# Pairs of heads on one 32-row strip of keys, and seven PSUM banks for the last element's second attention

## The chip, the cores and the metric

The kernel runs on one core of one Trainium2 chip. The metric is device time in microseconds (us) of one execution; lower is better. Times of several executions are given by their median.

## The reference

The input is `x` of shape 8 x 512 x 256 (elements, tokens, features). Four layers with residuals follow each other; all are in fp32. Cut to what matters:

```python
x = x + attn_a(layernorm(x))   # per token: 16 heads, a causal 64 x 64 table of q_i * k_j in each head
x = x + ffn(layernorm(x))      # 256 -> 1024 gated, 1024 -> 1024 twice, 1024 -> 256
x = x + attn_b(layernorm(x))   # causal attention over the 512 tokens, 16 heads of 16 features
x = x + ffn(layernorm(x))      # the same weights again

def attn_b(x):                                  # the "second attention"
    q, k, v = split(x @ W_attn + b_attn, 3)     # 256 -> 3 * 256
    s = q @ k.T / 4                             # per head, keys after the query masked
    return (softmax(s) @ v) @ W_proj + b_proj
```

## The kernel before, in words

Two streams of work are woven into one program. Stream A is the first attention of all eight elements (class `AttentionA`): 512 steps, 64 for each element, most of them on VectorE and GpSimd, with an exponential on ScalarE (L818) and a few matmuls. Stream B is the rest of each element, one element behind A: `ffn`, `attention_b`, `ffn`, most of it on TensorE. The order of the instructions on each engine is the order in which the source issues them. B is a generator that yields the worth of each piece of its work in units of its own; the main loop issues pieces of B after each third of an A step until B has done `total / 64` units for each A step, with `total = 309.5` units for an element. A has no more steps when B begins with the last element (`b = 7`), which is therefore processed by B alone.

TensorE does all matmuls, ScalarE copies their products out of PSUM and takes exponentials. PSUM has eight banks, in three pools: `ps_f` with five (stream B), `ps_qv` with two (queries and values of A) and the one tile `bank` of `ps_a` (A's small products, in halves). SBUF blocks of 128 x 2048 for B come from the pool `hp` with seven buffers, weights of B from `hwp` with three.

`attention_b` of one element goes through these parts:

- **Queries and keys** (L1187, copied out at L1208). Each head has 16 features and gets a strip of 32 partitions (`SLOT`), half of it zeros, so 16 heads fill four groups of 128 partitions (`BG = 4`). For queries (`j = 0`) and for keys (`j = 1`) there are four products of 128 x 512 each, two matmuls (`c`) in each product. The keys' four products are issued one by one, each followed by its copy.
- **Values** (L1225, copied at L1228): four products of 128 x 256.
- **Scores** `scores(g, j)` for the group `g` of four heads and the block `j` of 128 keys, with the width `w = 512 - 128 j` of queries: four matmuls, one per head, on four 32-row strips of the array, into four PSUM banks (L1242); four small matmuls that add the causal mask (L1246); four exponentials on ScalarE (L1249) into the SBUF tile `eb`, of which there is one.
- **Values' products** `values(g, j)`: four matmuls, one per head, on four 32-column strips, that add into the PSUM tile `pyb` of the group (L1254). After the last `j` of a group ScalarE copies `pyb` to `ytb` (L1263).
- Then the sums of the exponentials divide, the heads are turned back and projected, and `x` is updated.

The loop over the 16 pairs `(g, j)` issues, for each pair, the values' products of the pair before and then the scores of this pair:

```python
for j in range(NT):
    if before is not None:
        values(*before)
    es = scores(g, j)
```

The weights of queries and keys (tile `wbqk`, 1 MB for an element) are prepared once in `later_weights`, kept in the DRAM tensor `wbqk_d`, and loaded again for each element (L954).

Of the kernel before, what the change touches and what calls it, by code (L numbers as in the profile page):

```python
# [9 lines left out]
F32 = mybir.dt.float32  # L10
# [6 lines left out]
P = 128  # L17
EPS = 1e-5
NEG = -1e30
NB, S, D = 8, 512, 256  # L20
NT = S // P
DC = D // P
# [4 lines left out]
GW = GH * C  # L27
# [6 lines left out]

BH, HD, SLOT = 16, 16, 32
BG = BH * SLOT // P

FH = 1024
MC = FH // P
HB = 2048  # L40
# [3 lines left out]
def general_path(ctx: ExitStack, tc: tile.TileContext, k, t):  # L44
# [29 lines left out]
    nc.sync.dma_start(s3_sb, t.s3.broadcast_to([P, D]))  # L74
    wbqk_sb = wp.tile([P, DC, 2, BG * P], F32, name="g_wbqk")
    nc.sync.dma_start(wbqk_sb, t.w_bqk.rearrange("(c p) j f -> p c j f", p=P))
    bbqk_sb = wp.tile([P, 2, BG], F32, name="g_bbqk")
    nc.sync.dma_start(bbqk_sb, t.b_bqk)
# [3 lines left out]
    nc.sync.dma_start(wbp_sb, t.w_bp.rearrange("(c p) f -> p c f", p=P))  # L82
    bq_scaled = wp.tile([P, BG], F32, name="g_bqs")
    nc.vector.tensor_scalar_mul(bq_scaled, bbqk_sb[:, 0, :], HD**-0.5)
# [125 lines left out]
    def attention_b(xt):  # L210
        xnt = normed_block(xt)
        qk = hp.tile([P, 2, BG, S], F32, tag="h", name="g_qkb")
        for j in range(2):
            for g in range(BG):
                pp = ps.tile([P, S], F32, tag="pf", name="g_pqkb")
# [69 lines left out]
def fast_path(ctx: ExitStack, tc: tile.TileContext, k, t, flag):  # L285

    nc = tc.nc
# [3 lines left out]
    dram = ctx.enter_context(tc.tile_pool(name="dram", bufs=1, space=bass.MemoryType.DRAM))  # L291
# [8 lines left out]
    ps_qv = ctx.enter_context(tc.tile_pool(name="ps_qv", bufs=2, space=bass.MemoryType.PSUM))  # L300
    ps_a = ctx.enter_context(tc.tile_pool(name="ps_a", bufs=1, space=bass.MemoryType.PSUM))
    ps_f = ctx.enter_context(tc.tile_pool(name="ps_f", bufs=5, space=bass.MemoryType.PSUM))
# [7 lines left out]
    def block(name, dtype=F32):  # L310

        return hp.tile([P, HB], dtype, tag="h", name=name)
# [49 lines left out]
    def less_row(w, c, row, p0):  # L362

        ps = ps_f.tile([P, 2 * GW], F32, tag="pf", name="pfit")[:, : w.shape[-1]]
        nc.tensor.matmul(ps, ident, w, start=True, stop=False)
        nc.tensor.matmul(ps, from_rows[p0 : p0 + 1, c, :], row, start=False, stop=True)
        return ps

    def fit_qkv(g):

        wqv, wk = fitted[g]
        rows = (
            (wqv, last_rows[0:1, g * 2 * GW : (g + 1) * 2 * GW], 0),
            (wk, last_rows[32:33, g * GW : (g + 1) * GW], 32),
        )
        for w, row, p0 in rows:
            pss = [less_row(w[:, c], c, row, p0) for c in range(DC)]
            yield
            for c, ps in enumerate(pss):
                nc.scalar.copy(w[:, c], ps)  # L380
            yield
        nc.sync.dma_start(wqv_d[g].rearrange("p (c f) -> p c f", c=DC), wqv)
        nc.sync.dma_start(wk_d[g].rearrange("p (c f) -> p c f", c=DC), wk)
# [52 lines left out]
        nc.vector.tensor_scalar(over[0:1, 0:2], over[0:1, 0:2], 1.0, None, ALU.is_gt)  # L436

    w3_d = dram.tile([P, HB], F32, name="w3_d")
    wbqk_d = dram.tile([P, HB], F32, name="wbqk_d")
    wbvp_d = dram.tile([P, 2 * DC * D], F32, name="wbvp_d")  # L440

    nc.gpsimd.memset(rows_of_1[:, D:], 1.0)
# [2 lines left out]
    def later_weights():  # L445


        for j, row in enumerate((t.bo, t.b_bp)):
            nc.sync.dma_start(biases[j][:, :D], row)
        for g in range(1, NG):  # L450
            yield from fit_qkv(g)

        wbqk = block("wbqk").rearrange("p (c f) -> p c f", c=DC)
        rows = block("rows")
        w3 = block("w3").rearrange("p (c f) -> p c f", c=MC)
        wbvp = block("wbvp")[:, : 2 * DC * D].rearrange("p (j c f) -> p j c f", j=2, c=DC)
        n_qk = 2 * BG * P
        s3 = rows[:, n_qk + D : n_qk + 2 * D]
        nc.sync.dma_start(s3, t.s3.broadcast_to([P, D]))
        nc.sync.dma_start(w3, t.w3.rearrange("(c p) f -> p c f", p=P))  # L460
        nc.sync.dma_start(wbqk, t.w_bqkb.rearrange("(c p) j f -> p c (j f)", p=P))
        nc.sync.dma_start(wbvp[:, 0], t.w_bvb.rearrange("(c p) f -> p c f", p=P))
        nc.sync.dma_start(wbvp[:, 1], t.w_bp.rearrange("(c p) f -> p c f", p=P))
        nc.sync.dma_start(rows[0:1, :n_qk], t.w_bqk[D - 1 : D].rearrange("o j f -> o (j f)"))
        nc.sync.dma_start(rows[0:1, n_qk : n_qk + D], t.w_bv[D - 1 : D])
        yield
        for c in range(0, MC, 2):
            pair = w3[:, c : c + 2, :]
            nc.gpsimd.tensor_tensor(pair, pair, s3.unsqueeze(1).to_broadcast(list(pair.shape)), ALU.mult)
            yield  # L470
        for w, off, width in ((wbqk, 0, 2 * GW), (wbqk, 2 * GW, 2 * GW), (wbvp[:, 0], 0, D)):
            row = rows[0:1, n_qk if width == D else off :][:, :width]
            pss = [less_row(w[:, c, off : off + width], c, row, 0) for c in range(DC)]
            yield
            for c, ps in enumerate(pss):
                nc.scalar.copy(w[:, c, off : off + width], ps)
            yield

        nc.sync.dma_start(w3_d, w3.rearrange("p c f -> p (c f)"))
        nc.sync.dma_start(wbqk_d, wbqk.rearrange("p c f -> p (c f)"))  # L480
        nc.sync.dma_start(wbvp_d, wbvp.rearrange("p j c f -> p (j c f)"))
        yield
        yield from bound_scores()
# [18 lines left out]
    bank = ps_a.tile([P, 2, GW], F32, name="bank")  # L502
# [674 lines left out]
    def attention_b(b, xt, nx, after):  # L1177
        yield from nx.wait(NT - 1)
        xnt = nx.t
        qk = [block(f"qkb_{b}_{j}").rearrange("p (g s) -> p g s", g=BG) for j in range(2)]  # L1180
        w = weights.take().rearrange("p (c j f) -> p c j f", c=DC, j=2)
        for j in range(2):
            pps = [None] * BG

            def products(g, toks):
                for c in range(DC):
                    nc.tensor.matmul(  # L1187
                        pps[g][:, toks],
                        w[:, c, j, g * P : (g + 1) * P],
                        xnt[:, c, toks],  # L1190
                        start=(c == 0),
                        stop=(c == DC - 1),
                    )

            if j == 0:

                for g in range(BG):
                    pps[g] = ps_f.tile([P, S], F32, tag="pf", name=f"pqkb_{b}_{j}_{g}")
                    products(g, most)
                    if g % 2:  # L1200
                        flush()
                        yield 2
                yield from nx.wait(NT)
            for g in range(BG):
                if j > 0:
                    pps[g] = ps_f.tile([P, S], F32, tag="pf", name=f"pqkb_{b}_{j}_{g}")
                products(g, slice(0, S) if j > 0 else last)
                nc.scalar.activation(qk[j][:, g, :], pps[g], AF.Copy, scale=HD**-0.5 if j == 0 else 1.0)  # L1208
                yield 1.8 if j > 0 else 0.6
            if j == 0:  # L1210
                weights.ahead()

        vs = block(f"vb_{b}").rearrange("p (i h s) -> p i h s", i=NT, h=BH)
        yts = block(f"ytb_{b}").rearrange("p (g q) -> p g q", g=BG)
        exps = block(f"eb_{b}").rearrange("p (h q) -> p h q", q=S)
        rest = block(f"yb_{b}")
        y2 = rest[:, : 2 * D].rearrange("p (n h d) -> p n h d", n=2, h=BH)
        yt2 = rest[:, 2 * D : 4 * D].rearrange("p (n c q) -> p n c q", n=2, c=DC)
# [16 lines left out]
        heads = range(P // SLOT)  # L1235
        slots = [slice(h * SLOT, (h + 1) * SLOT) for h in heads]

        def scores(g, j):
            keys, w = slice(j * P, (j + 1) * P), S - j * P
            scs = [ps_f.tile([P, S], F32, tag="pf", name=f"psb_{b}_{g}_{j}_{h}")[:, :w] for h in heads]  # L1240
            for h in heads:
                nc.tensor.matmul(  # L1242
                    scs[h], qk[1][slots[h], g, keys], qk[0][slots[h], g, j * P :], start=True, stop=False
                )
            for h in heads:
                nc.tensor.matmul(scs[h][:, :P], k.ident16, k.tmask16, start=False, stop=True)  # L1246
            es = [exps[:, h, :w] for h in heads]
            for h in heads:
                nc.scalar.activation(es[h], scs[h], AF.Exp)  # L1249
            return es  # L1250
# [14 lines left out]
        before = None  # L1265
        for g in range(BG):
            for j in range(NT):
                if before is not None:
                    values(*before)
                es = scores(g, j)  # L1270
                if j == 0:
                    yt = ps_f.tile([P, S], F32, tag="pf", name=f"pyb_{b}_{g}")
                before = (yt, g, j, es)
                yield 6 - j
# [81 lines left out]


    each = NT * NG * NU
    total = 309.5
    ET = mybir.EngineType  # L1360
    with tc.manual_schedule(engines={ET.PE, ET.DVE, ET.Activation, ET.Pool}):
        a = AttentionA()
# [4 lines left out]
        weights = None  # L1367
# [104 lines left out]
```

## Time and profile before

| | |
|---|---|
| median of 3 runs | 3988.24 us (3980.57 to 3991.68) |
| profiled execution, first to last instruction | 3990.8 us |
| the same execution's own time | not given apart; its span lies within the runs |
| mean granted TensorE clock | 0.849 |
| busy: TensorE, VectorE, GpSimd, ScalarE | 76%, 85%, 77%, 59% of the span |
| stream A's last output is copied by ScalarE at | 3687.1 us |
| second attention of the last element: first product of the queries | 3801.7 us |
| its last exponential; its last copy of `ytb` | 3871.8 us; 3872.9 us |

Times within the profile are us from its first instruction. The page of the profile lists groups of instructions by source line; the timeline lists single instructions or merged rows of equal ones, with the idle time of the engine before them and what ended it in brackets. One product of fp32 appears as two matmul records. The busy share is a mean over the whole span and hides the two stages: until 3687 us both streams run, after it B alone.

### The profile page before, as it was taken

How to read it: one execution, taken by the hardware profiler on the slowest of the kernel's cores; microseconds unless marked ns; L12 is line 12 of the kernel's file. 1: busy time of each engine (PE TensorE's matmuls, PEld its weight loads, DVE VectorE, ACT ScalarE, POOL GpSimd, SP SyncE). 2: the span in 40 equal slices, each digit the busy share in tenths (PEclk: the TensorE clock that was granted, in tenths of full speed). 3: DMA queues.
4: the chain of work that ended last, by engine and by line, in shares of the span. 5: the costliest groups of instructions: out<-in, count | busy, mean ns of one | idle time of the engine just before them, and what ended most of it. 6: DMA issues, size and time to landing. Idle time of an engine off the chain costs nothing.

```text
span 3990.8 us, 37932 instructions
## 1 busy us (share of the span) xinstructions
PE 3039.9 (76%) x12464; PEld 2055.2 (52%) x12464; DVE 3375.9 (85%) x3776; ACT 2341.3 (59%) x3156; POOL 3077.9 (77%) x3040
## 2 busy tenths in 40 slices
PE   5653487687877878678876878778787778778988
PEld 2231264365634656356643656346553556446847
DVE  7999988998899888998899988998989888996115
ACT  3444475576665675666755766666755767565342
POOL 6888878887888788887788887887888877886111
PEclk7556599798987988888987989879898889879999
DMA  8766777577776877768775877668776677767304
GB/s 229 182 137 137 159 197 158 124 191 189 199 154 139 196 191 178 148 163 202 200 157 118 208 186 194 149 142 213 174 190 143 160 182 206 158 129 211 116 28 169
DMA packets 118346, 669.24 MB, mean 168 GB/s; under 512 B 12662, under 2 KB 31865, under 8 KB 43643
## 3 DMA queue, kind: packets, MB, share of 16 engines
q0 software_dynamic: 78336, 570.46, 63.2%
q1 hardware_dynamic: 39804, 96.27, 6.7%
q8 instruction: 101, 1.65, 0.2%
q14 instruction: 105, 0.86, 0.1%
HBM read 254.07 MB, written 9.96 MB: 66 GB/s over the span
## 4 chain that ended last, share of the span: by engine, by line
DVE 38%; PE 18%; POOL 14%; DMA 13%; ACT 8%; issue 8%; SPq 0%; ACTq 0%; POOLq 0%; DVEq 0%
DVE red L865 15%; DMA w<-w 13%; DVE w L828 10%; PE ph L1140 5%; ACT w L818 4%; POOL w L804 3%; POOL w L839 3%; DVE ws L828 3%; PE pqkb L1187 3%; POOL acc L872 3%; DVE w L804 2%; DVE ws L804 2%; POOL h L1056 2%; POOL w L834 2%; DVE acc L876 2%
## 5 line engine op out<-in xcount | busy, mean ns | idle before, releaser
L818 ACT ACTIVATE w<-w 128x2048 f32<-128x2048 f32 x384 | 733.8, 1912 | 659.2 <-POOL w L804 461.3
L1140 PE MATMUL ph<-h,hidden 128*128 128x512 f32 x4096 | 1042.9, 411 | 72.4 <-POOL h L1056 42.9
L804 POOL TENSOR_TENSOR w<-k 128x1024 f32<-128x1024 f32 x512 | 1077.4, 2104 | 7.7 <-ACT k L782 7.1
L1140 PEld LDWEIGHTS ph<-h,hidden 128*128 128x128 f32 x4096 | 792.3, 195 | 275.3 <-POOL h L1056 53.8
L828 DVE TENSOR_TENSOR w<-w,qv 128x1024 f32<-128x1024 f32 x768 | 898.8, 1211 | 22.4 <-ACT w L818 22.4
L865 DVE TENSOR_REDUCE red<-w 128x128 f32<-128x1024 f32 (+1 forms) x384 | 601.3, 1566 | 178.0 <-DMA w<-w 93.6
L839 POOL TENSOR_TENSOR w<-w 128x1024 f32<-128x1024 f32 x256 | 643.7, 2514 | 82.9 <-DMA w<-w 82.3
L834 POOL DMA_DIRECT2D w<-w x384 | 337.9, 880 | 349.0 <-issue 121.1
L872 POOL TENSOR_TENSOR acc<-acc,red 128x256 f32<-128x256 f32 (+1 forms) x640 | 471.2, 736 | 142.7 <-DVE red L865 122.0
L865 DVE TENSOR_REDUCE red<-ws 128x256 f32<-128x2048 f32 (+1 forms) x256 | 435.4, 1742 | 0.0
L766 PE MATMUL qv<-wqv,xnta 128*128 128x512 f32 x512 | 299.7, 716 | 104.6 <-DVE ws L828 95.4
L1072 PE MATMUL pw<-xnt,gate 128*128 128x512 f32 (+2 forms) x1152 | 301.8, 422 | 21.7 <-ACT silu L1048 16.1
L828 DVE TENSOR_TENSOR ws<-ws,qv 128x1024 f32<-128x1024 f32 (+3 forms) x512 | 294.3, 635 | 27.6 <-ACT ws L818 27.6
L804 DVE TENSOR_TENSOR w<-qv,k 128x1024 f32<-128x1024 f32 x256 | 301.1, 1218 | 3.6
L804 DVE TENSOR_TENSOR ws<-qv,k 128x1024 f32<-128x1024 f32 (+3 forms) x512 | 299.5, 646 | 0.2 <-issue 0.2
L888 PE MATMUL bank<-ident,acc 128*128 128x128 f32 x256 | 62.4, 333 | 284.5 <-ACT k L781 278.6
L818 ACT ACTIVATE ws<-ws 128x1920 f32<-128x1920 f32 x128 | 231.5, 1808 | 80.7 <-DVE ws L804 80.1
L1072 PEld LDWEIGHTS pw<-xnt,gate 128*128 128x128 f32 x1152 | 230.8, 215 | 76.2 <-ACT silu L1048 20.4
L1249 ACT ACTIVATE eb<-psb 128x256 f32<-128x256 f32 (+3 forms) x512 | 182.1, 443 | 139.1 <-PE psb L1246 138.6
L1166 PE MATMUL pof<-w,h 128*128 128x256 f32 x1024 | 244.9, 392 | 22.8 <-ACT h L1105 22.8
L1105 ACT ACTIVATE h<-ph,s_sb 128x512 fp32r<-128x512 f32 (+1 forms) x256 | 171.2, 688 | 151.1 <-PE ph L1140 149.7
L876 DVE RECIPROCAL acc<-acc 128x256 f32<-128x256 f32 x128 | 222.9, 1741 | 11.9 <-POOL acc L872 11.9
(149 smaller groups left out, 4846.4 us busy)
## 6 DMA issues: line engine op xcount, KB each, us to landing
w<-w POOLq DMA_DIRECT2D x384, 1024.0 KB, 7.8
hidden<-in_h POOLq DMA_DIRECT2D x128, 1024.0 KB, 7.9
gate<-in_w12p POOLq DMA_DIRECT2D x32, 1024.0 KB, 9.1
w<-w_d SPq DMA_DIRECT2D x16, 1024.0 KB, 11.5
wqv<-wqv_d SPq DMA_DIRECT2D x31, 512.0 KB, 4.6
wo<-in_wo SPq DMA_DIRECT2D x32, 256.0 KB, 7.6
wbqk<-wbqk_d SPq DMA_DIRECT2D x8, 1024.0 KB, 9.0
w<-in_h SPq DMA_DIRECT2D x8, 1024.0 KB, 8.6
```

Of the source, the lines that this page charges most:

```text
L766: nc.tensor.matmul(qv.rearrange("p j f -> p (j f)"), xnt[:, c, :], wqv[:, c, :], start=(c == 0), stop=(c == DC - 1),)
L804: eng.tensor_tensor(e, rows(q).to_broadcast(shape), columns(kt[:, 0]).to_broadcast(shape), ALU.mult)
L818: nc.scalar.activation(e, e, AF.Exp, scale=C**-0.5)
L828: nc.vector.tensor_tensor(ev, e, columns(qv[:, 1]).to_broadcast(list(e.shape)), ALU.mult)
L834: nc.gpsimd.dma_start(w[:, :2048], w[:, 2048:], accum_op=ALU.add)
L839: nc.gpsimd.tensor_tensor(w[:, :1024], w[:, :1024], w[:, 1024:2048], ALU.add)
L865: nc.vector.tensor_reduce(red, self.columns_of(w, n, off, nsq), AX.X, ALU.add)
L872: nc.gpsimd.tensor_tensor(rows, rows, part.rearrange("p a (x i) -> p a x i", i=n), ALU.add)
L876: nc.vector.reciprocal(acc[:, 0, :], acc[:, 0, :])
L1072: nc.tensor.matmul(pj[:, toks], w[:, m % 4, j, c, :], xs[:, p, c, toks], start=(p == 0 and c == 0), stop=(p == 1 and c == DC - 1),)
L1140: nc.tensor.matmul(pss[j], w[:, j, c, :], h_in(p, c), start=(p == 0 and c == 0), stop=(p == 1 and c == MC - 1),)
L1166: nc.tensor.matmul(po, h(0, c)[:, i * P : (i + 1) * P], w3[:, c, :], start=(c == 0), stop=False)
```

## The change

Four things change, all in the second attention.

1. Two heads share one 32-row strip of keys: the first in the upper 16 rows, the second in the lower 16. The queries keep one strip per head, with zeros in the half where the other head's keys lie. The keys then fill two groups (`KG = 2`) in place of four; the order of the heads in the weights of values and of the output projection is permuted to fit. `wbqk` has 768 columns for each `c` in place of 1024. The number and shape of the scores' matmuls stay.
2. For the last element (`alone`) the scores take seven PSUM banks in turn: four of `ps_f`, two of `ps_qv` and `bank`. The other elements keep `ps_f`.
3. For the last element there are two `eb` tiles, used in turn with `j`.
4. For the last element each pair's scores are issued before the values' products of the pair before it.

`total` goes from 309.5 to 305.9 units: two yields of 1.8 for the keys' groups are gone.

```diff
+KG = BH * HD // P
+QK = BG * P + KG * P
...
-        for j in range(2):
-            pps = [None] * BG
+        for j, groups in enumerate((BG, KG)):
+            pps = [None] * groups
...
-                        w[:, c, j, g * P : (g + 1) * P],
+                        w[:, c, (j * BG + g) * P : (j * BG + g + 1) * P],
...
-        exps = block(f"eb_{b}").rearrange("p (h q) -> p h q", q=S)
+        alone = b == NB - 1
+        exps = [block(f"eb_{b}_{n}").rearrange("p (h q) -> p h q", q=S) for n in range(1 + alone)]
...
+        taken = [0]
+
+        def score_bank(name):
+
+            n, taken[0] = taken[0] % 7, taken[0] + 1
+            if not alone or n < 4:
+                return ps_f.tile([P, S], F32, tag="pf", name=name)
+            if n < 6:
+                return ps_qv.tile([P, S], F32, tag="qv", name=name)
+            return bank.rearrange("p j f -> p (j f)")
+
         def scores(g, j):
             keys, w = slice(j * P, (j + 1) * P), S - j * P
-            scs = [ps_f.tile([P, S], F32, tag="pf", name=f"psb_{b}_{g}_{j}_{h}")[:, :w] for h in heads]
+            scs = [score_bank(f"psb_{b}_{g}_{j}_{h}")[:, :w] for h in heads]
...
-                    scs[h], qk[1][slots[h], g, keys], qk[0][slots[h], g, j * P :], start=True, stop=False
+                    scs[h], qk[1][slots[h], g // 2, keys], qk[0][slots[h], g, j * P :], start=True, stop=False
...
-            es = [exps[:, h, :w] for h in heads]
+            es = [exps[j % len(exps)][:, h, :w] for h in heads]
...
-                if before is not None:
+                if before is not None and not alone:
                     values(*before)
                 es = scores(g, j)
+                if before is not None and alone:
+                    values(*before)
...
-    total = 309.5
+    total = 305.9
...
+    heads = [8 * (g // 2) + 2 * s + g % 2 for g in range(BG) for s in range(P // SLOT)]
+    order = np.concatenate([np.arange(h * HD, (h + 1) * HD) for h in heads])
```

More of the change, by code (lines that the diff above doesn't have):

```diff
@@ L438, in fast_path @@
     w3_d = dram.tile([P, HB], F32, name="w3_d")
-    wbqk_d = dram.tile([P, HB], F32, name="wbqk_d")
+    wbqk_d = dram.tile([P, DC * QK], F32, name="wbqk_d")
     wbvp_d = dram.tile([P, 2 * DC * D], F32, name="wbvp_d")
@@ L451, in later_weights @@
             yield from fit_qkv(g)
-        wbqk = block("wbqk").rearrange("p (c f) -> p c f", c=DC)
+        wbqk = block("wbqk")[:, : DC * QK].rearrange("p (c f) -> p c f", c=DC)
         rows = block("rows")
@@ L456, in later_weights @@
         wbvp = block("wbvp")[:, : 2 * DC * D].rearrange("p (j c f) -> p j c f", j=2, c=DC)
-        n_qk = 2 * BG * P
+        n_qk = QK
         s3 = rows[:, n_qk + D : n_qk + 2 * D]
@@ L460, in later_weights @@
         nc.sync.dma_start(w3, t.w3.rearrange("(c p) f -> p c f", p=P))
-        nc.sync.dma_start(wbqk, t.w_bqkb.rearrange("(c p) j f -> p c (j f)", p=P))
+        nc.sync.dma_start(wbqk, t.w_bqkb.rearrange("(c p) f -> p c f", p=P))
         nc.sync.dma_start(wbvp[:, 0], t.w_bvb.rearrange("(c p) f -> p c f", p=P))
-        nc.sync.dma_start(wbvp[:, 1], t.w_bp.rearrange("(c p) f -> p c f", p=P))
-        nc.sync.dma_start(rows[0:1, :n_qk], t.w_bqk[D - 1 : D].rearrange("o j f -> o (j f)"))
-        nc.sync.dma_start(rows[0:1, n_qk : n_qk + D], t.w_bv[D - 1 : D])
+        nc.sync.dma_start(wbvp[:, 1], t.w_bpf.rearrange("(c p) f -> p c f", p=P))
+        nc.sync.dma_start(rows[0:1, :n_qk], t.w_bqkl)
+        nc.sync.dma_start(rows[0:1, n_qk : n_qk + D], t.w_bvl)
         yield
@@ L470, in later_weights @@
             yield
-        for w, off, width in ((wbqk, 0, 2 * GW), (wbqk, 2 * GW, 2 * GW), (wbvp[:, 0], 0, D)):
-            row = rows[0:1, n_qk if width == D else off :][:, :width]
+        for w, off, width in ((wbqk, 0, BG * P), (wbqk, BG * P, KG * P), (wbvp[:, 0], 0, D)):
+            row = rows[0:1, off if w is wbqk else n_qk :][:, :width]
             pss = [less_row(w[:, c, off : off + width], c, row, 0) for c in range(DC)]
@@ L1180, in attention_b @@
         qk = [block(f"qkb_{b}_{j}").rearrange("p (g s) -> p g s", g=BG) for j in range(2)]
-        w = weights.take().rearrange("p (c j f) -> p c j f", c=DC, j=2)
-        for j in range(2):
-            pps = [None] * BG
+        w = weights.take().rearrange("p (c f) -> p c f", c=DC)
+        for j, groups in enumerate((BG, KG)):
+            pps = [None] * groups
             def products(g, toks):
@@ L1195, in attention_b @@
             if j == 0:
-                for g in range(BG):
+                for g in range(groups):
                     pps[g] = ps_f.tile([P, S], F32, tag="pf", name=f"pqkb_{b}_{j}_{g}")
@@ L1203, in attention_b @@
                 yield from nx.wait(NT)
-            for g in range(BG):
+            for g in range(groups):
                 if j > 0:
@@ L1420, with queries_and_keys @@
     wqv = np.stack([a[A + n].reshape(D, NG, GW) for n in ("Wq", "Wv")], axis=2).reshape(D, NG, 2 * GW)
+    heads = [8 * (g // 2) + 2 * s + g % 2 for g in range(BG) for s in range(P // SLOT)]
+    order = np.concatenate([np.arange(h * HD, (h + 1) * HD) for h in heads])
+    def queries_and_keys(v):
+        q = np.zeros(v.shape[:-1] + (BH, SLOT), v.dtype)
+        for n, h in enumerate(heads):
+            q[..., n, h % 2 * HD :][..., :HD] = v[..., h * HD : (h + 1) * HD]
+        return np.concatenate([q.reshape(v.shape[:-1] + (BH * SLOT,)), v[..., D : 2 * D]], axis=-1)
+    w_qkf, b_qkf = queries_and_keys(w_attn), queries_and_keys(b_attn)
     def with_row(w, row):
@@ L1432 @@
         "wkb": with_row(a[A + "Wk"], a[A + "bk"]),
-        "w_bqkb": with_row(w_qk.reshape(D, 2, BG * P), b_qk.reshape(2, BG * P)),
-        "w_bvb": with_row(w_attn[:, 2 * D :], b_attn[2 * D :]),
+        "w_bqkb": with_row(w_qkf, b_qkf),
+        "w_bqkl": w_qkf[-1:],
+        "w_bvb": with_row(w_attn[:, 2 * D :][:, order], b_attn[2 * D :][order]),
+        "w_bvl": w_attn[-1:, 2 * D :][:, order],
+        "w_bpf": a[B + "W_proj"][order],
         "b_at": np.stack([a[A + n].reshape(HID // P, P).T for n in ("bq", "bk", "bv")], axis=1),
```

## The prediction

> **What bounds the kernel now.** First the page's slices, for the stages:
>
> ```profile
> PE   5653487687877878678876878778787778778988
> DVE  7999988998899888998899988998989888996115
> ACT  3444475576665675666755766666755767565342
> ```
>
> VectorE falls from 8 or 9 tenths to almost nothing in the last three slices, 300 us, where TensorE stays at 9, 8, 8. Then the same cut as a table (window, its length, busy us and number of instructions of PE, PEld, DVE, ACT, POOL, granted clock, DMA share, GB/s):
>
> ```profile
> 0.00:3687.00 3687.00, 2760.20 (x11124) 1849.06 (x11125) 3293.47 (x3672) 2236.41 (x2946) 3028.39 (x2959) 0.84 0.73 173
> 3687.00:3991.00 304.00, 279.75 (x1342) 206.19 (x1340) 82.42 (x104) 104.91 (x210) 49.49 (x82) 0.96 0.31 106
> ```
>
> While both streams run, VectorE is 89% busy and GpSimd 82%. The last element's 304 us are TensorE's: what it loses there goes into the time one for one. So I read the two stages apart.
>
> In the last stage, the timeline of TensorE shows one of the four groups (a pair's scores, their masks, then the values' products):
>
> ```profile
> 3833.61 1.14 PE L1242 MATMUL psb<-qkb,qkb 32*128 32x512 f32 x8
> 3834.69 0.40 PE L1246 MATMUL psb<-tmask,ident 128*128 128x128 bf16 x4
> 3835.67 2.51 PE L1254 MATMUL pyb<-eb,vb 128*32 128x512 f32 x8 [0.58 <-ACT eb L1249]
> 3838.11 0.93 PE L1242 MATMUL psb<-qkb,qkb 32*128 32x384 f32 x8
> 3838.97 0.40 PE L1246 MATMUL psb<-tmask,ident 128*128 128x128 bf16 x4
> 3839.84 1.98 PE L1254 MATMUL pyb<-eb,vb 128*32 128x384 f32 x8 [0.47 <-ACT eb L1249]
> ```
>
> and that of ScalarE the same group:
>
> ```profile
> 3835.01 2.06 ACT L1249 ACTIVATE eb<-psb 128x512 f32<-128x512 f32 x4 [0.71 <-PE psb L1246]
> 3839.30 1.64 ACT L1249 ACTIVATE eb<-psb 128x384 f32<-128x384 f32 x4 [2.21 <-PE psb L1246]
> 3842.72 1.21 ACT L1249 ACTIVATE eb<-psb 128x256 f32<-128x256 f32 x4 [1.79 <-PE psb L1246]
> 3845.30 0.79 ACT L1249 ACTIVATE eb<-psb 128x128 f32<-128x128 f32 x4 [1.36 <-PE psb L1246]
> 3846.58 0.59 ACT L1263 COPY ytb<-pyb 128x512 f32<-128x512 f32 x1 [0.49 <-PE pyb L1254]
> 3847.87 2.06 ACT L1249 ACTIVATE eb<-psb 128x512 f32<-128x512 f32 x4 [0.71 <-PE psb L1246]
> ```
>
> The two take turns: a group's period is 12.86 us (3835.01 to 3847.87), of which ScalarE works 6.29. TensorE looks busy for 11.2, but the values' 2.51 is not their own speed: they run at the pace of the exponentials (in the first pair their weights are loaded at 3822.87, 3823.30, 3823.78, 3824.28, the spacing of the exponentials). What they need when nothing holds them shows earlier, where stream A delayed them:
>
> ```profile
> 1668.06 1.06 PE L1254 MATMUL pyb<-eb,vb 128*32 128x512 f32 x8
> 1669.06 0.93 PE L1242 MATMUL psb<-qkb,qkb 32*128 32x384 f32 x8
> ```
>
> Likewise 0.85, 0.64 and 0.42 for 384, 256 and 128 columns (at 1142.32, 683.81 and 710.59).
>
> For the stage of both streams, the chain that ended last around one projection of queries and keys (start, us):
>
> ```profile
> 2498.60 11.35 PE pqkb L1187 x36
> 2512.53 1.73 PE pqkb L1187 x4
> 2517.99 1.72 PE pqkb L1187 x4
> ```
>
> and the same stretch as a window:
>
> ```profile
> 2498.00:2521.00 23.00, 21.39 (x67) 12.50 (x68) 19.29 (x19) 11.68 (x20) 20.14 (x18) 0.87 0.60 137
> ```
>
> The chain runs through this projection, but VectorE is busy for 19.3 and GpSimd for 20.1 of the 23 us: little lies behind it.
>
> **What the Trainium skill says.** "TensorE: Matmul & The Clock Gate", Part 3, gives three 32-column tiles of 512 columns 2.38 times the speed, four 32-row tiles 3.07 times. The trace agrees: four values' products take 1.06 us, where one full product of 512 columns takes 0.86 (1.72 for two). The same part has matmuls start and end strictly in order: a score that waits for its bank holds the masks and values behind it. "TensorEngine Tiling (Array Packing)", under PSUM pressure, has row tiles write different banks; here four scores take four banks, and with `pyb` five are used, so the next scores cannot start before the exponentials have read. "PSUM — Partial Sum Buffer", under engine and sequencer instructions, has ScalarE's queue strictly in order; the waits of the window above show 11.3 us of ScalarE behind key and query products, with A's exponentials after them.
>
> **The change part by part.**
>
> *Keys, last element.* Two products of two matmuls go, at 1.72 us each (copies come at 3811.87, 3813.59, 3815.30, 3817.02, with ScalarE idle 1.12 between): TensorE is the bound, so -3.4 us. Their two copies of 0.60 ran beside it.
>
> *Order, banks and tiles, last element.* Moved: for each pair 4 score matmuls, 4 masks, 4 exponentials, ahead of 4 values' products; no DMA and nothing on SP's or GpSimd's queue. On ScalarE the copy of `ytb` now stands behind the next group's first exponentials. The added wait: with seven banks in turn, a pair's fourth score needs the bank of the first exponential of the pair before. Behind it wait the masks and the values. I walk one group with: scores to first mask 1.07, 0.86, 0.65, 0.43 us (`j` = 0 to 3); masks 0.40; first mask to exponential 0.33; four exponentials 1.98, 1.56, 1.13, 0.72 (start to start, from the spacings); exponential to values 0.15; last value to next scores 0.97, 0.76, 0.53, 0.30. With the old order this walk gives 52.7 us from the first score to the last copy of `ytb`; the trace has 52.5 (3820.37 to 3872.88). With the new order, from the first exponential of a group at 0:
>
> - ScalarE does `j=0` until 1.98, the copy until 2.57. TensorE meanwhile ends the last values of the old group (0.39), and the scores of `j=1`: the fourth starts at 0.65 (bank), masks end at 1.90. Exponentials of `j=1` 2.57 to 4.13.
> - Values of `j=0`: the last can start at 2.13, done 3.10. Scores of `j=2`: masks from 3.75; exponentials 4.13 to 5.26, at once.
> - Values of `j=1` need the exponential of 4.13: last at 4.28, done 5.04. Scores of `j=3`, mask 5.47, exponentials 5.80 to 6.52.
> - Values of `j=2` after the masks (5.87), done 6.43. Scores of the next group, mask 7.50, exponentials from 7.83.
>
> So a period of 7.83 for 12.86. Lead-in (table load and first scores, 1.8) is as now; three periods save 15.1, the last group 4.4 (12.1 from its first exponential to its copy, 7.7 in the walk): -19.6 us with rounding. Floor: ScalarE never idle, 5.98 a group, about -27. Ceiling: values that don't pack, 11.2 a group, -6.7. What is late next is TensorE and ScalarE by turns (gaps of 0.54 and 1.31 on ScalarE).
>
> *The eighth `hp` block.* `yb` now lies where `xnt` of this element lay, whose last reader is the values' projection, over 30 us before `yb` is written. Nothing. The next gate weights (9.1 us to land) were hidden under the scores' 52 us; 33 cover them still.
>
> *Keys, elements 0 to 6.* 3.4 us of TensorE at full clock (3.9 at 0.87), two copies of 0.60, and the 0.25 MB less in the load of `wbqk` (prefetched). The steps of A around it stand as before, within one step. The window can shrink only by what VectorE (3.7) and GpSimd (2.9) have idle, and part of that is waits of their own. Bounds 0 and 3.9; I take 1.4 for each, -10 us for seven; to -20 in the range. Below nothing too: shifted collisions, a rival below. The smaller preparation (under 2 us, once, beside A's first steps): nothing.
>
> Sum: 3990.8 - 3.4 - 19.6 - 10 = 3957.8 on the span. The median of the runs stands 2.6 below that span: **3955 us**.
>
> **Rivals.**
>
> 1. *The last stage alone gains* (both streams stay bound by VectorE and GpSimd): for it the 89% of VectorE; against it the chain through the products. 3990.8 - 23.0 - 2.6 = 3965.
> 2. *All of the keys' time comes back*: 7 x 3.9 = 27, 3938. Against it GpSimd's 20.1 of 23 us.
> 3. *The values don't pack in the new order* (they alternate with 32-row scores and full masks): -6.7 in place of -19.6, 3968. Against it the 1.06 us, which stood between full products and scores.
> 4. *Slower.* With two fewer products the exponentials of the second attention reach ScalarE's queue sooner, ahead of A's exponentials, and VectorE waits; place: elements 0 to 6, after the keys. ScalarE waited 138.6 us for scores in the whole run, 23.6 of it in the last element, so 16 in each of the others. To end 0.3% slower it must cost over (23 + 12) / 7 = 5 us an element; at 7 it gives 3988 + 49 - 23 = 4014. Against it: VectorE is 92 and 100% busy in the two stretches after the projection (41.2 of 45 and 43.9 of 44 us) without help.
> 5. *The change does not do what it says*: scores of the last element wait for the copy of `pyb`'s bank after all, 0.6 in three groups: under 2 us, in the range.
>
> **How the numbers follow.** Forecast (both gains) 0.60; only the last stage 0.20; all of the keys' time 0.08; no packing 0.08; slower 0.04. The range is 3936 (rival 2 and a median 2 below) to 3974 (rival 3 and a median 6 above: runs differ by 11). A measurement of this kernel tells about 0.3%, 12 us, from no change: faster below 3976, 0.92; same 0.05; slower 0.03.
>
> **What would show it.** After: the last element's keys in two products; its scores to the last `ytb` copy in about 33 us, ScalarE's group starts 7.8 apart, first values about 1.1 us where they were 2.5; the stage of both streams ending 0 to 20 us earlier than 3687. Wrong, if the values still take 2 us, if the fourth score waits longer than its bank, or if that stage ends later than before.

## The result, and the profile after

| | before | after |
|---|---|---|
| median | 3988.41 us (20 runs) | 3981.26 us (20 runs, 3975.01 to 3989.28) |
| profiled execution, first to last instruction | 3990.8 us | 3978.1 us (its own time 3979.9) |
| last copy of stream A by ScalarE | 3687.1 | 3700.1 |
| first product of the last element's queries | 3801.7 | 3813.2 |
| from there to the end | 189.1 us | 164.9 us |

The change is faster by little: ratio 0.9983 (0.9976 to 0.999), 7 us. The forecast was 3955, its range ended at 3974. The last element gained what was forecast; the stage before it, in which both streams run, lost about half of that again.

Both halves show in the slices and the windows (0 to the end of A, and the rest; columns as before):

```profile
PE   5553487687866877678876878768787778777998
DVE  7999988998899988988989888898889889898115
```

```profile
0.00:3700.00 3700.00, 2728.80 (x11068) 1852.45 (x11069) 3295.51 (x3672) 2236.06 (x2936) 3029.66 (x2959) 0.83 0.73 172
3700.00:3978.00 278.00, 260.22 (x1334) 198.84 (x1332) 82.42 (x104) 102.99 (x208) 49.41 (x82) 0.97 0.33 115
```

The lonely stage went from 304 to 278 us. The shared stage went from 3687 to 3700, with TensorE's busy time 31 us down and VectorE's unchanged (3293 and 3296).

Part of the third group of the last element on TensorE, then ScalarE's group starts (`...` stands for rows left out):

```profile
3846.35 1.06 PE L1268 MATMUL pyb<-eb,vb 128*32 128x512 f32 x8 [0.23 <-ACT eb L1263]
...
3848.32 0.89 PE L1268 MATMUL pyb<-eb,vb 128*32 128x384 f32 x8
3849.14 0.50 PE L1256 MATMUL psb<-qkb,qkb 32*128 32x128 f32 x8
3849.57 0.40 PE L1260 MATMUL psb<-tmask,ident 128*128 128x128 bf16 x4
3849.90 0.64 PE L1268 MATMUL pyb<-eb,vb 128*32 128x256 f32 x8
```

```profile
3836.60 2.06 ACT L1263 ACTIVATE eb<-psb 128x512 f32<-128x512 f32 x4 [1.19 <-PE psb L1260]
3838.53 0.62 ACT L1277 COPY ytb<-pyb 128x512 f32<-128x512 f32 x1
...
3844.23 1.09 ACT L1263 ACTIVATE eb<-psb 128x512 f32<-128x512 f32 x2 [1.18 <-PE psb L1260]
...
3858.84 0.59 ACT L1277 COPY ytb<-pyb 128x512 f32<-128x512 f32 x1 [0.49 <-PE pyb L1268]
```

In this group, the third, the values' products take 1.06, 0.89 and 0.64 us, no longer the exponentials' pace. The first pair's values took 2.37 us in the first group, where they start right behind their exponentials (3829.81 and 3829.02), and 1.34 in the second and fourth. A group starts every 7.6 us (3836.60 to 3844.23) where it was 12.86. TensorE's idle time in the third group is gone but for 0.23.

The chain at one projection of queries and keys, and its window:

```profile
2506.21 8.76 PE pqkb L1189 x24
2514.97 0.86 PE bank L763 x4
2515.83 1.72 PE qv L768 x4
2517.55 4.34 PE pqkb L1189 x16
```

```profile
2506.00:2530.00 24.00, 20.95 (x66) 13.38 (x66) 19.69 (x20) 10.03 (x18) 19.84 (x19) 0.82 0.63 145
```

From the first query product to the last key product it is 15.7 us where the chain before shows 21.1 (2498.60 to 2519.71), so the projection itself did not get longer. The loss is elsewhere. Between the last copy of `yb` (second attention) and the next element's first query product lies the stretch of the two feed-forward networks. Before (1709 to 2035, then its attention) and after (1707 to 2039, then its attention):

```profile
1709.00:2035.00 326.00, 261.28 (x1022) 198.93 (x1020) 285.55 (x331) 218.61 (x263) 266.51 (x276) 0.89 0.76 186
1572.00:1709.00 137.00, 104.03 (x515) 52.65 (x514) 129.01 (x136) 79.60 (x136) 116.34 (x101) 0.84 0.69 146
```

```profile
1707.00:2039.00 332.00, 262.50 (x1034) 200.16 (x1032) 289.88 (x334) 220.62 (x264) 271.96 (x281) 0.89 0.74 181
1575.00:1707.00 132.00, 96.20 (x496) 48.90 (x497) 125.35 (x133) 77.11 (x132) 112.05 (x97) 0.84 0.71 152
```

The attention won 5 us and the feed-forward stretch, in which no line was edited, lost 6, with 4.3 us more of VectorE in it: work of A has moved from one into the other.

### The profile page after: what moved, and what is told of

The parts are those of the page before. It is cut to its first block, busy times and chain, and to the rows that moved or that the text cites. A ratio compares the mean times of both kernels' runs of the same rounds, so it can differ in the third digit from the quotient of the medians.

```text
span 3978.1 us, 37799 instructions
## 1 busy us (share of the span) xinstructions
PE 2989.0 (75%) x12400; PEld 2051.3 (52%) x12400; DVE 3377.9 (85%) x3776; ACT 2339.1 (59%) x3144; POOL 3079.1 (77%) x3040
## 4 chain that ended last, share of the span: by engine, by line
DVE 35%; PE 20%; POOL 15%; DMA 12%; ACT 9%; issue 8%; SPq 0%; POOLq 0%; ACTq 0%; DVEq 0%
DVE red L867 14%; DMA w<-w 11%; DVE w L830 9%; PE ph L1142 6%; ACT w L820 4%; POOL w L806 3%; POOL w L841 3%; POOL acc L874 3%; DVE ws L830 3%; DVE ws L806 3%; PE pqkb L1189 2%; DVE w L806 2%; PE pof L1168 2%; PE pw L1074 2%; POOL w L836 2%
## 5 line engine op out<-in xcount | busy, mean ns | idle before, releaser
L1142 PE MATMUL ph<-h,hidden 128*128 128x512 f32 x4096 | 1064.1, 418 | 88.3 <-POOL h L1058 57.9
L1142 PEld LDWEIGHTS ph<-h,hidden 128*128 128x128 f32 x4096 | 808.5, 199 | 291.6 <-POOL h L1058 67.1
L768 PE MATMUL qv<-wqv,xnta 128*128 128x512 f32 x512 | 279.4, 673 | 73.1 <-DVE ws L830 63.0
L820 ACT ACTIVATE ws<-ws 128x1920 f32<-128x1920 f32 x128 | 231.5, 1809 | 131.5 <-DVE ws L806 131.2
L1074 PE MATMUL pw<-xnt,gate 128*128 128x512 f32 (+2 forms) x1152 | 288.8, 409 | 22.6 <-ACT silu L1050 16.8
L1263 ACT ACTIVATE eb<-psb 128x512 f32<-128x512 f32 (+3 forms) x503 | 180.3, 450 | 129.2 <-PE psb L1260 128.8
L1168 PEld LDWEIGHTS pof<-w,h 128*128 128x128 f32 x1024 | 202.6, 200 | 80.6 <-ACT h L1107 45.4
```

Source lines behind the costliest of these rows:

```text
L768: nc.tensor.matmul(qv.rearrange("p j f -> p (j f)"), xnt[:, c, :], wqv[:, c, :], start=(c == 0), stop=(c == DC - 1),)
L820: nc.scalar.activation(e, e, AF.Exp, scale=C**-0.5)
L1074: nc.tensor.matmul(pj[:, toks], w[:, m % 4, j, c, :], xs[:, p, c, toks], start=(p == 0 and c == 0), stop=(p == 1 and c == DC - 1),)
L1142: nc.tensor.matmul(pss[j], w[:, j, c, :], h_in(p, c), start=(p == 0 and c == 0), stop=(p == 1 and c == MC - 1),)
L1168: nc.tensor.matmul(po, h(0, c)[:, i * P : (i + 1) * P], w3[:, c, :], start=(c == 0), stop=False)
```

## The experiments

Runs are given as ratio to the kernel before, timed beside them, with the interval. For each profile I measured the mean feed-forward stretch (six of them, as above), the mean second attention (first query product to last `yb` copy, elements 0 to 6), and where A's last copy stands; and I counted A's steps in them by ScalarE's exponentials (one for each step). Before: 326.6 and 137.3 us, 42 or 43 and 21 or 22 steps, 3687.1. After: 333.9 and 132.6 us, 43 and 21 steps throughout, 3700.1.

My theory: the pace. The main loop spreads A's 64 steps evenly over the `total` units of B. The yields of the source add up to 114.2 of 309.5 units in the second attention before, and to 110.6 of 305.9 after: 23.6 and 23.1 steps. So half a step goes over to the feed-forward stretches, as the counts have it (42.5 and 43 on average), and the steps behind the keys fall on other products than before. The rivals: the last element's buffers hurt A; or less TensorE work disturbs A whatever the pace.

### Keys alone

```diff
-        alone = b == NB - 1
+        alone = False
```

> The shared strips of keys and total = 305.9 alone; the last element keeps the old order, five banks and one tile. Pace theory (taking 3.6 units from each element moves A's steps out of the second attention, where a step costs about 6.2 us, into the feed-forward stretches, where it costs about 7.7): stream A ends 8 to 15 us later than before's 3687, the last element's keys give back 3.4 to 5, so 3992 to 3999, slower than before by 0.1 to 0.3%. Rival 'the last part hurts A' (the loss comes from the last element's tiles and banks): A ends at 3687 or earlier, 3975 to 3985.

1.0032 (1.002 to 1.0044), 4005.27 us: **slower than before**, by slightly more than expected (the kernel before had 3992.68 beside it). A's last copy at 3701.9, stretches 333.7 and 133.1. The loss sits in the keys and their pace.

### The last element alone

Before's keys and `total`, with parts 2 to 4 of the change.

> Before's keys and total = 309.5; only the last element's seven banks, two tiles and order. Pace theory: A ends as before (3687), the scores of the last element take 30 to 31 us in place of 50.7: -20, so 3966 to 3970, faster than the full change. Rival 'the last part hurts A': A ends about 12 us later, 3978 to 3982.

0.9941 (0.9928 to 0.9955), 3970.45 us. A's last copy at 3687.6, half a microsecond from before. The rival of the buffers falls, and these three parts of the change beat the whole: the two intervals do not touch.

### Two pauses after the keys

```diff
+            if j > 0:
+                for _ in range(BG - KG):
+                    yield 1.8
...
-    total = 305.9
+    total = 309.5
```

> The full change, but after the keys two empty yields of 1.8 units each and total = 309.5, so that A keeps its share of steps beside each stretch of B. Pace theory: feed-forward stretches of an element take 326 us as before (332 to 335 in the changed kernel), A ends at 3675 to 3687, total 3952 to 3966. Rival 'less TensorE work itself disturbs A' (shifted collisions whatever the pace): A ends 8 to 15 us late again, 3976 to 3984.

0.9926 (0.9912 to 0.9939), 3962.46 us. Stretches 326.2 and 136.4, with the step counts of the kernel before; A's last copy at 3677.0: 23 us before the changed kernel's, 10 before the old one's. Its two stages:

```profile
0.00:3677.00 3677.00, 2740.87 (x11068) 1842.44 (x11069) 3293.32 (x3672) 2229.55 (x2932) 3029.51 (x2959) 0.84 0.73 173
3677.00:3958.00 281.00, 260.76 (x1333) 197.99 (x1332) 82.36 (x104) 103.07 (x208) 49.45 (x82) 0.97 0.32 114
```

No instruction of TensorE differs from the changed kernel's but for its place. So the pace cost the changed kernel 23 us, by A's end and by the ratios alike, and "less TensorE work disturbs A" falls.

### Each key group made twice

```diff
-        for j, groups in enumerate((BG, KG)):
+        alone = b == NB - 1
+        twice = 1 if alone else 2
+        for j, groups in enumerate((BG, KG * twice)):
...
-    total = 305.9
+    total = 309.5
```

> The full change, but elements 0 to 6 make each of the two key groups twice (four products and four copies, as before), with total = 309.5. Pace theory: stream A as before (3687), last element as changed: 3963 to 3968. It stands 0 to 10 us above the run with pauses by what the saved products are worth beside A; if both are equal, the products were worth nothing there. Rival 'less TensorE work itself disturbs A': this one is faster than the run with pauses by some 12 us.

0.9941 (0.9927 to 0.9954), 3968.5 us, A's last copy at 3683.1. The saved products are worth 6 us in seven elements by the medians and by A's end, if anything: the two intervals overlap.

### Four pauses, pauses elsewhere, another phase

Four pauses is the run above with `range(2 * (BG - KG))` and `total = 313.1`.

> As the run with two pauses after the keys, with four of them (7.2 units) and total = 313.1: A gets 1.5 steps of each 64 more beside the second attention than in the changed kernel. Share theory (a step of A costs more beside the feed-forward products than beside the second attention): feed-forward stretches of 320 to 325 us, second attention 138 to 142, A ends 0 to 10 us before the two-pause run's 3677, total 3950 to 3962. Alignment theory (which step of A falls on which product matters, not how many): no order to expect; 3955 to 3985.

0.9908 (0.9891 to 0.9926), 3952.2 us; stretches 324.9 and 137.1 with 42 and 22 steps everywhere, A's last copy at 3666.6. Against the changed kernel one step has moved (by the yields 0.94; the expectation's 1.5 left out that the rest of the attention is repaced too): 9.0 us less for 4.5 more, and (9.0 - 4.5) x 7 = 31.5 is close to the 33.5 by which A ends earlier. This is no constant price of a step: the two pauses, half a step, had already brought 7.7 less for 3.8 more.

Then the two pauses, one in each feed-forward network in place of after the keys:

```diff
         for _ in range(2):
             flush()
             yield 1
+        yield 1.8
...
-    total = 305.9
+    total = 309.5
```

> The full change, total = 309.5, but the two empty yields of 1.8 stand one in each feed-forward network, after its gate products, in place of after the keys. Share theory: the shares are no better than in the changed kernel; feed-forward stretches 332 to 338 us, 3976 to 3986. Rival 'the pace total alone' (309.5 units an element are right whatever stands in them): as the two-pause run, 3958 to 3966.

0.9955 (0.994 to 0.997), 3971.49 us: stretches 334.3 and 130.7, as the share theory has them, but the total lies below its range. The number of units alone does not do it; the place of the pauses matters.

And the same shares with B set back by two steps of A:

```diff
-                while 3 * spent * each < total * (3 * (n - each - 11) + part + 1):
+                while 3 * spent * each < total * (3 * (n - each - 13) + part + 1):
```

> The full change with total = 305.9, stream B set back by two more steps of A (constant 13 for 11), which shifts every product of B by half of A's four-step cycle and changes no share. Share theory: feed-forward stretches stay at 332 to 336 us, the tail grows by about 10 us, 3985 to 3995. Alignment theory: the stretches change by 5 us or more either way, most likely back to 325 to 328, 3945 to 3965.

0.9974 (0.9966 to 0.9982), 3978.12 us. Stretches 332.7 and 131.5, each about 1.1 us shorter than in the changed kernel: far from the 5 us of the alignment theory. But the total lies below the share theory's range. A ends at 3689.8, 10 us earlier than in the changed kernel, and that pays back the longer tail (121.4 us from A's last copy to the last element's first query product, in place of 113.1).

### Where it stops

Eight pauses (`total = 320.3`), and the four pauses' units spread over the scores (`yield 6.45 - j`, `total = 313.1`):

> Eight empty yields of 1.8 units after the keys and total = 320.3: about one step of A more than with four pauses moves from beside the feed-forward products to beside the second attention. If the exchange rate of the runs so far holds on (9.0 us off the feed-forward stretch for 4.5 us more in the attention): 41 and 23 steps, A ends some 30 us before the four-pause run's 3667, 3920 to 3930. If the second attention is full (VectorE already busy there for 105 of 108 us), the step costs as much as it saves: 3945 to 3960.

1.0043 (1.003 to 1.0057), 4006.42 us, above both ranges. 41 and 23 steps as planned in all elements but the last one counted, but the feed-forward stretch does not fall (328.3) and the attention grows to 142.1. The exchange rate does not hold below 42 steps.

> The four pauses' 7.2 units spread over the 16 pairs of the scores (6.45 - j in place of 6 - j), total = 313.1, nothing after the keys. Share theory: what counts is the units of the second attention, not the place in it; feed-forward stretches of 323 to 327 us, 3947 to 3958. Rival (A needs a stretch of its own behind the keys' products): 3962 to 3975.

0.9916 (0.9902 to 0.9929), 3955.31 us; 323.8 and 139.5. The interval overlaps that of the four pauses: the place within the attention matters little.

Is it the number of steps with a floor, or the phase? Three runs: four pauses and eight pauses with B set back by two steps (13 for 11), and six pauses (`total = 316.7`).

> Four pauses, total = 313.1, stream B set back by two steps of A: same numbers of steps beside each stretch, half a cycle shifted. Numbers count: feed-forward stretches of 323 to 327 us, 3947 to 3957. Alignment counts: stretches off by 5 us or more, 3965 to 3990.

0.9875 (0.9856 to 0.9894), 3938.18 us, **the lowest ratio of the study**, though its interval just touches that of the four pauses, and below both ranges. Still 42 and 22 steps, but 318.3 and 141.0 us; A's last copy at 3650.9. One of its stretches, and the attention before it:

```profile
1699.00:2018.00 319.00, 259.39 (x1026) 194.54 (x1025) 284.57 (x325) 215.99 (x262) 267.49 (x276) 0.90 0.77 188
1557.00:1699.00 142.00, 102.49 (x505) 51.24 (x504) 130.50 (x142) 78.46 (x133) 115.64 (x103) 0.80 0.67 143
```

The same VectorE work as with 326 us (284.6 against 285.6 busy), and 6 us less of VectorE's idle time (34.4 against 40.4). The theory of numbers alone falls too; the alignment theory had the feed-forward stretches right and the total wrong.

> Eight pauses, total = 320.3, stream B set back by two steps. Numbers count, with a floor: stretches of 323 to 332 us as at eight pauses, attention 141 to 144, 3998 to 4010. Alignment counts: the 41 steps beside the feed-forward stretch show their worth, 315 to 322 us, 3920 to 3960.

1.0008 (1.0001 to 1.0015), 3991.26 us, in neither range; 318.3 and 147.7. The setback takes 10 us off the stretch and puts 6 on the attention; 41 steps are again no cheaper than 42.

> Six pauses, total = 316.7. Numbers count, with a floor: between four (3952) and eight (4006), 3960 to 3990, the feed-forward stretches flat at 323 to 328 and the attention longer. Alignment counts: no order, 3940 to 4010.

0.9973 (0.9964 to 0.9981), 3976.77 us; 326.8 and 138.1, between four and eight pauses. The first two stretches hold 43 steps, the other four 41. Both ranges have this total, so it decides nothing.

So the number of steps does not settle how long a stretch is: which step of A falls on which product counts at equal numbers (324.9 and 318.3 us with 42 steps in every stretch). The kernel before says the same. Its last three stretches hold 43 steps, as all of the changed kernel's do; two of them take 324.6 and 323.6 us, no longer than those with 42 (325.9 to 326.6), where the changed kernel's take 332.0 to 336.1. That the number counts on its own is not shown, since each run that changed it also moved the steps against the products. Why 41 steps are no cheaper than 42 stays open too, and whether other paces would help the kernel with the old keys was not tried.

### The last element's three parts

All three are made on the kernel with two pauses, one run each; only the timeline of the last element is used, not the total. The figures are from the first exponential to the last copy of `ytb` (before 50.7, after 30.4 us). In five banks:

```diff
-            if not alone or n < 4:
+            if True:
```

> The two-pause run with the last element's scores in the five banks of ps_f alone; two tiles and the new order stay. By the walk with a bank free again after four: a group's period is 10.2 us (12.86 before, 7.6 in the changed kernel), first exponential to last copy of ytb 40.6 us. If banks don't matter (the order alone does it): 30 to 31 us.

40.8 us (3807.75 to 3848.57), group starts 10.15 us apart:

```profile
3818.27 2.06 ACT L1266 ACTIVATE eb<-psb 128x512 f32<-128x512 f32 x4 [1.43 <-PE psb L1263]
3820.19 0.62 ACT L1280 COPY ytb<-pyb 128x512 f32<-128x512 f32 x1
3821.55 1.64 ACT L1266 ACTIVATE eb<-psb 128x384 f32<-128x384 f32 x4 [0.74 <-PE psb L1263]
3824.20 1.21 ACT L1266 ACTIVATE eb<-psb 128x256 f32<-128x256 f32 x4 [1.01 <-PE psb L1263]
3826.20 0.78 ACT L1266 ACTIVATE eb<-psb 128x128 f32<-128x128 f32 x4 [0.80 <-PE psb L1263]
3828.42 2.06 ACT L1266 ACTIVATE eb<-psb 128x512 f32<-128x512 f32 x4 [1.43 <-PE psb L1263]
```

ScalarE is kept waiting at every pair, 15.3 us in all, and TensorE's scores wait for exponentials 26 times, 12.3 us (in the changed kernel once, 0.8 us): with four banks in turn each score needs the bank of the same head in the pair before. The order with two tiles brings half of the gain, the banks on top of it the other half.

With seven banks and two tiles but the old order (values first):

> The two-pause run with the last element's values before the next scores, as before; seven banks and two tiles stay. By the walk the banks and tiles then bring nothing: group starts 12.9 us apart, first exponential to last copy of ytb 50 to 51 us.

50.9 us (3804.42 to 3855.28), group starts 12.82 us apart: banks and tiles bring nothing without the order.

With one tile (`range(1)` for `range(1 + alone)`):

> The two-pause run with one tile of exponentials in the last element; seven banks and the new order stay, so a pair's exponentials wait for the values' products of the pair before. By the walk with that wait: ScalarE's group starts 9.9 us apart (7.6 in the changed kernel), first exponential to last copy of ytb 39.3 us. If the second tile does nothing: 30 to 31 us.

50.4 us (3811.36 to 3861.81). The expectation had the wait the wrong way round: with one tile the next pair's exponentials are written before the values read, so the values take the next pair's exponentials (this run changes that part of the computation) and wait for them. The order is then undone. So the new order needs the second tile for its result, whatever the tile is worth in time; the wait that this run was meant to price was not measured.

## Why the prediction was wrong, point by point

- **Keys, last element**: forecast -3.4, measured -4.7 (15.2 us from the first query product to the first value product before, 10.5 after). The mechanism was right, and 3.4 is the products: the run of the last element alone kept the old keys at a granted clock of 1.00 and took 13.9, which is 3.4 more than 10.5. The rest is the clock, which the forecast had no term for: granted 0.66 and 0.77 in 3800 to 3806 before, 1.00 in 3811 to 3817 after.
- **Order, banks, tiles**: forecast a period of 7.83 (its own terms add up to 7.80) and -19.6, measured 7.6 and -20.3 (50.7 to 30.4). Right, and for its reasons: the five-bank run and the old-order run fell where the same walk put them (10.2 and 12.9 forecast, 10.15 and 12.82 measured).
- **Eighth block, prefetch**: costed at nothing; the end after the scores took 118.7 us where it took 117.9. Right.
- **Keys, elements 0 to 6**: forecast -10, measured +13.0 at A's end (+11.5 at the last element's first query product). **This step failed**, at the sentence that "the steps of A around it stand as before, within one step". Half a step of 64 is all that the change of `total` moves from beside the attention to beside the feed-forward products. That lies within the "one step", and together with the new places of the steps it was worth 23 us. I costed the removed work, and no term stood for the re-pacing. With the pace held by two pauses A ends at 3677.0, -10.1. That it meets the forecast for the work itself is in part luck: with as many products as before, at the same pace, A ends at 3683.1, which is 4.0 us before the old kernel's end without any product saved.
- **Rival 4** (slower) had the sign of A's end, but neither the size nor the place: it spoke of 5 to 7 us an element after the keys, and measured are 13 / 7 = 1.9. The second attention, where its exponentials were to hold A, got shorter. It asked what it takes to end slower by 0.3%; 1.9 us an element sufficed to take half of the last element's gain.
- **The sum**: 33 us were forecast, 7 came. With two pauses in place of the new pace it is 29 to 30 us (0.9926 of 3990.8).

## What to carry to other kernels

In a program that weaves two streams by a hand-set pace, taking work out of one stretch moves the other stream's work into the rest, and onto other products. The change of the pace constant is an edit of its own: time it apart from the work that was removed. A price of a step that one pair of runs gave (9.0 us against 4.5) did not hold for the next, so it is no more than a guess to be measured. Price a stage in which two engines take turns by walking its waits from measured bursts: it held here within 1 us for three kernels, and failed for the one whose wait was drawn the wrong way round. Time the parts of a bundled change apart: here three of the four parts alone, and the whole with a pause in it, both beat the bundle.

## What the runs showed of the hardware

- Four values' products on 32-column strips took 1.06 us also where they alternate with 32-row scores and full-array masks (third group above), as when they stood between full products.
- The granted clock at the start of the last element's projection differs between profiles of nearly the same work (0.66 and 1.00 above), worth 1.3 us there. In the profile of the four pauses with B set back it was 0.50 and 0.56 in the first 6 us, and the same products as in the changed kernel took 13.2 us where that took 10.5.
